# An attention and feed-forward kernel whose result is stored tile by tile, with a new order of its instructions

## The chip, the cores and the metric

The kernel runs on one core of one Trainium2 chip. The core has five engines that work side by side, each on its own stream of instructions: TensorE (PE, matrix products and transposes, with PEld for its weight loads), VectorE (DVE), ScalarE (ACT), GpSimd (POOL) and SyncE (SP), which here only issues transfers. The metric is the device time of one execution in microseconds (us), taken as the median of several runs. The kernel before takes 428.0 us (three runs: 428.0, 427.61, 428.92).

## What is computed

Eight batches of 512 tokens with 512 features pass a cross-attention to 64 memory tokens and then a gated feed-forward block of width 2048, both with a residual. Every linear of the block quantises its input by rows to 8 bits and its weight to three values:

```python
def _rmsnorm(x, g):
    return g * (x * rsqrt(mean(x * x, axis=-1, keepdims=True) + EPS))
def _act_quant(x):
    scale = 127.0 / clip(max(abs(x), axis=-1, keepdims=True), 0.0001, None)
    return clip(round(x * scale), -128, 127) / scale
def _ternary_quant(w):
    s = mean(abs(w))
    return round(tanh(w / (s + EPS))) * arctanh(s)
def _linear_bit(x, w, g):
    return einsum('bsd,od->bso', _act_quant(_rmsnorm(x, g)), _ternary_quant(w))
def _ffn(x):
    h = silu(_linear_bit(x, w1, g1)) * _linear_bit(x, w2, g2)
    return _linear_bit(h, w3, g3)
x = x + _xattn(_layernorm(x), ctx, mask)     # softmax(scores) @ ctx, masked
x = x + _ffn(_layernorm(x))                  # x: 8 x 512 x 512 float32
```

## The kernel before, in words

A batch is four tiles of 128 tokens (tokens on the 128 partitions, 512 features each). A tile goes through these steps, and the names are those that the profile shows:

- Input. `load_x` (lines 473 to 485) brings `mem`, `both` and `x`, 1 MB for a batch, on the queue SP.
- Attention, first half, `pre`: statistics of each tile (`st`, lines 560 and 562), small columns (567), the normalised `t` (582 on ACT or 586 on POOL or DVE), its half-precision copy `xh` (590 on ACT, 591 on DVE) and the remainder (592), a transpose to `xT` (298), and the scores `psc` (602). The maximum is taken off the scores (628 and after).
- Attention, second half, `expo` and `post`: exponential, sum (659), two half-precision parts of the weights `ph` (668 on ACT, 669 on DVE), their transpose to `pT` (298), the product `po` (683), and the addition to `x` (691).
- Quantised input, `quantise_x`: the centred `xm` (721, 725), its squares (731), times the gain (`z`, 736), largest value (741), columns of scales (749 to 766), the two quantised halves (799 on ACT, 800 on POOL or DVE), and the transpose to `zT` (298).
- Feed-forward, `up` and `gate`: for each tile two halves of 1024 columns. `linear` (883) makes `p` in PSUM from `zT` and the weights `w1T` or `w2T`, eight matmuls of 128x512 for a half. SiLU into `h` on ACT (899), the product with the second linear on DVE (927), squares on ACT (932), gain on POOL or DVE (940), then largest value (964), columns (968 to 976), quantisation of `h` (997 on ACT, 999 on POOL), and two transposes to `hT` (1002).
- Down projection, `down_quarter`: 16 matmuls in four quarters into `pd` (825), the addition `x` <- `pd` on DVE (835), and the store. The very last tile goes through `down_last` in two halves of the columns (854, stores at 866).

The transposes `xT`, `zT`, `pT`, `hT` and `mT` are DMA transposes and stand on the queue SP with all loads and stores (for batch 0, and for the last tile, PE transposes instead, and DVE or ACT copies the result out at line 309). An instruction on SP waits for its source at the head of the queue, and everything behind it waits with it.

Before the batches stand the weights: `load_w`, `measure_w` (353, mean of the absolute values), `arctanh` (434), and `quantise_w` (386 on ACT, POOL or DVE; PE transposes; the copy to `w1T`, `w2T`, `w3T` at 390 on DVE, four for each weight).

The program is a plan: `op` notes for each step which engine may do it, what it reads and what it writes. `up` calls `between` four times a tile, where one quarter of the down projection of a tile three places back (`LAG = 3`) and pieces of the attention of later batches (`during`) are noted. The order in which the steps are at last issued, and the engine of each step that has a choice, come from the string `ORDER`, which packs a list of 16-bit codes: the step's number times four, plus the way chosen. `Plan.order` unpacks it, and the loop at the end of the kernel issues the steps one by one; each engine executes its own in that order. Buffers of SBUF and PSUM are assigned by the same order: nine 1 MB buffers `big` hold weights, `x` and `h`; PSUM has three buffers `mm` for `p`, `po` and transposes, one `o` for `pd`, one `a` for `psc`.

The store before, for a tile that isn't the very last, is at lines 839 to 842: the batches 0 to 6 are stored whole, after their fourth tile, and the tiles 0 to 2 of batch 7 one by one.

Of the kernel before, what the change touches and what calls it, by code (L numbers as in the profile page):

```python
# [87 lines left out]
class Plan:  # L88
# [19 lines left out]
    def op(self, engine, cost, run, writes, reads, table=None, other=()):  # L108

        me = len(self.ops)
        deps = set()
# [6 lines left out]
        for b, part in map(pair, writes):  # L120
# [28 lines left out]


ORDER = """
c-jTQedKy+q5$yo@|^eQob#M>o^#G~UY3@Y?~m_~mM$$_y0o;kv@~?-($LV*(9*qHS{k~vG&D4{S3{SEhW==1XlUqOEnONKS{fQ!8d_R
f`lF@cem)c>QkVi1q!1OQa#WtmQU!`oMe2nrQ4#8uDpMg<p<+~=s!|CmNu{VXm7(g?h3-;Ux=r<{4%MJ;G^9VFn$&>8^oJCphZLbl)KB
QIs2bI$BlOqQXH=A4QFnSkPpCEZhMrOz>R;$BHKS(ikp3k-r{2;TdPnW47@egL)RZ03-%}GdPUq+oHKxy0p8h*^p%V0+dQewtLMQ1TsV
V)Wzo3^a#XxpWQ*?p;mIh3b7MT(a8N>j3L1RXw-=p{Roc*3AOvpr-1O0nuNmu9$^C!AWpXey_!mMb-PPqkprr%*Ubed_<Ev7~{=~pJkZ
0Ri1qA~lR+jN|%(;Yg&beSYW*c4M>a!i{E*)DzLip+}b(F-QR9=Ir51R3xy^M>s(HRc0m!@S4TnI7}X_L&$vWJ};b**!O4TA;z?K^#n&
&zKqaCG$R00DopWU?}$3-?42lWV&F)WWk#4vtKhgFl7ep$Kb$p_&!)MBQ^ozY>OX&HS-12VaM#JV8b@qEz@PMpv||~5m<vUn1LO$Wko^
aCZG(COj`I0GY1J42|qA@W0LF!U?Ihh#2x#0Ce3DqP|vVX$g(t>74FQF*@7IK6CTW-&9i_lu<r;vP-HL6ci_NEY>7RxW%k5Y*n%(xXZF
HY*(10}PjF=mTv0fI8(U-VY@L0uG4Nz7;2rJ^y22a&p8@13um?9#1!e9eA+E>)`2z0Xw*Ye~PzM99!oB4l0Dv?&aaB$PPbtPNK%A>_ge
wV45OPB<#X%6^5QuVft}HY_f;)3>xSmiEk{kv^Xo6pHRiVUPI09CH;#yo^7zrWBa#yL!i*f`2uFV~U92W%(?#k7<SN<rxfF<_|R$PbsB  # L160
}egRsliclL|=0UzQzxPE%$p)<N^O8oP-#^6}#LUdBeTRJ09{+zR!&XN<jQXXbL?J2zx#zr}-Oa^E>X&J(N(0^J_6KKe&z9<wHKhzo=^=
%lG&sAK~Xhf`4*Rekj)ksOI<-KjQLyLn!haf$&42z>m3=^eRq;_xKWj;?v?n_#I#8D`JK3^Plofe!_LcwKU>q!XNpiu#sv)34P8d<drb
yqvH2`SBwZV{wy@a8$ac5%8Qtk@5)p7nxFGnEs1~Q-wG*t!T(HH^G$T;FG5@dVp-hqq7s$P{FZ<4P#MVyk&-AeE{S4HxbR8wA&zAzUIi
jH#gsUa3sPK&sX3`7hT=_#t9RiS!c%-zcOp^$A^Z;?5!+}iHlz=Qw(ufVq;G_s&=J~VUTR86-3v)!DZNTn=_noLln|2+;#`V}C;292#J
!jok78Dwi0`N;aVi$XAH<nxh#gcxTdANH#f4;xWz<4dloQYLT`H<j-bqNgihmW~RjVSBKS%$k?xlxx7i;1ag>p@*i#HKSJuxEN(nr!vh
SCg0Wl`#jL>h=UIU)7rP(l)x=VDD>iVJZi-sOy(lp<0~p2~HpE;r=0e34U9T1v}TIG0y)QNqfvq>}WI`_hL}TPjPhN>(CrSzX9ixg&*2
Oxdaf={t!iznAAqMCnOcxuWLesM1ina#dX@Z8-{uQd7yxDWxFil(aID{#(i@9i=aK<gz@Kwn|r7$}?#o$F(M`$O&zyY~+?wmACR(+AD9
AfzpCE*oOt>Tlo%qN?tiAOXVqNbV^C<M`ZwCAW(Afr0mqVvX>J|Q7$U4@Tu%oQ7b8Z<y|=st4awbmG_i{`o8jO1;CnekSTbANv*E56{v
l#i116)hC>Cykz&B9V#6`?;7mEg2b{pH{+SZO3q;xzifRP@#Guqr<<ylDQKRZcIjC#ptfaK08iz4BR8ug8x>gz{;8jVf8TF!+VMZINSv
3QbFsDw{u^KUE))3aziB*B2mW5bLs|DD%(pnWpv<0leqgq$z*3|k4)?o)`wGo`c9=xhE*i@rhPMgDmwm?O=REc&{=h|0lRXeLoxPoJ?0  # L170
axnhYC|t-6Rn}H;Z5DZnYz&S@T9fWwR(UL?V_HwwmMgP>Jiqoi~iK^YF?{reU;M3`a^AMPnFVMwSoE#>{;K!7j0nuL7i&9)7n~7k7+<(
YfCMvU$lw7(^pzYn`wKitmX8LCh9NxN9tC4)puGJMGdI$^@85gUW~og(%;oO#zBjtiZ<1OwnSI`sLl1fo<LpgW38yCQ4OuoK>If%hYnT
-mGp!DiT0iz(`Wk8s-uTK)ZW*t`c-@CBdv=*GHzPWC>eGAu61;zxAh(x=rz5suTc`+^sY|yzJc`{%A<u2QNyg8OTDM}Q4!V5ve7_yv_Y
ThuLd%PsAAl8${6W2V}w?E+8CpOvC-?spY)-D(EuIwlO8hwI_o2YLIotEszFfPc%YOqb+&rK*rFY37zn9G(wG`!BWs4}N3=&X<AC0vjd
MnEb7kzDxr2>Y^f1;&!rU1f<ELor#L&;s-pQGw`80rWMa0OPWAlQbd9pG_28+hTpiE>goTr&JW=_tSm`(G0ls7&!n#RE(=2r$~wT*9#q
&YYC#?CC5cV}rFjlZCi@q_VK1DHkgYV6H|fh}y7%!3)4cOzmpEMmQwM>C6W#@ULRB`dVr=Bqh1TV~8mSUKD=KQ`lf*F2e@m<c_pr}VNF
v4Ax&o7T{}SShP&rOc5zvcAM2zFH5bgVScxD&mZp#}S;h($@c)bF*d*&4u-axiL$4ZPu-f)x~GCY%Z<5wJ@XB*4*HgRj^*H9$uOYe6xy
H%PQcDSv4zG*ID8|zM4;`V<qv;Y+Ds`Y^^Y~?xtvMth@Ca>lGtwh__b7{kipO?W_;no>RtA9JgxtVXmzz9^t+-z`wv-JjRs!u%h<U+Tj
WYZrpycpP0fDe!&2%7~vEy*$ErthF!K}IE@KD;HG`EYwi)Z>^QFD(3!Y<+`vh@iCcJWPw~*6;I<9yh%>{l_Qp=zqI<%3dyUUH?xbw!?%
gXE?Hj)1ihaQer(^#E*WIz*#!H8?M>eu!Hnyj3%X!D{+65ch8GGgy?TMYWR}ONg_80b-_Q3hhox8uW+m2^1?5#a?4$jdH?U56)tM<|9*  # L180
-N`_FWiAmIcNK1pWMEEv6t@2so5+0TN}GccW)o;tG#lg4safJ+DW;hbF>@o*-1KQH{)Df=s<#;g7fNp=5(B#({!)y8z<|eoR|~3H+SOX
owZYRpLWZ=IKOi9<m$9tL~`!U!Op+BEmCr_ZplrPo||{mE+)h&J7u@%v`N>!yK6T?D$c--xF0wnIg`3mAjIvvQTL5IAaC6w>9|9;;f&m
koAjE_kZj!xp~=pT5|8A)lvg4n@^A|t^2X%p=E#y1y$Z>a7lJ)NN?w`7T#>BF$Q!%Fi@Ph*AyxA4WJ79BjWo#AOSoIo@V+IX_h&Npnq=
i2$jpn7rZ*uiZ|!ZpDd~C@zvsP@wzu<sK{{TS{G3$%e<GiFSCS-s67hNjcqx+fY41kvMDmVg?xnq`_aG+%y|TCW1|IS&-i!AnLvP_tJn
Ub*S1;zxNZiYKDSzozy<dA9@8Hcz&O3Sw67gGp+CO=}^={tTi}?w!?p;0NXZ*MR!EgI_Z|mp$xZm*~-j5#b1Apvi{m@VNHNWfce9^!9M
<4n<KkDE7sh<c=e&5ggg&-Nc_!Ix^&-`*w@aKLpDEeRdU;7RJKm5JF@+-l+e$#*WpZfphm;Gum^3%c7uLWzL3NC&o*!Z&m1li#3Hv=)q
1tb^;Fff93&<Z9&JHSCScnNU03Fbj0Bw;5AgKiKBJ`VmEd=e~zT@VdlgJm!bQo%kL1?lh*<b&^nQt-Fn9^8UNI0%#BBcQ`)z=cv+4>I8
}Yy_h)8^UlJyo9+h7L3DkxC&4>3Ae%9Fdm$Od{_x*;WRu4^Dq`(f-qc!)vy*e!g|;YTVXuxhN-X}_QF4eg|Htk!(zAzOW`WqhU@SU?!t
X|3{T-X{D0au@s|
"""  # L190
# [8 lines left out]
def kernel(  # L199
# [620 lines left out]
    def down_quarter(state, q):  # L820
        b, c, hT, f, po = state

        def run():
            for n in range(q * NH // 4, (q + 1) * NH // 4):
                T.matmul(  # L825
                    po(), hT()[:, n * P : (n + 1) * P], w3T()[:, n, :],
                    start=(n == 0), stop=(n == NH - 1),
                )
# [9 lines left out]
        view = out[b].rearrange("(p c) d -> p c d", c=NC)
        if b == B - 1:
            op(DMA, (475, 650, 600), lambda: Q.dma_start(view[:, c, :], xt()[:, c, :]), [], [(xt, c)])  # L840
        elif c == NC - 1:
            op(DMA, (475, 650, 2000), lambda: Q.dma_start(view, xt()), [], [xt])
# [301 lines left out]
```

## Time and profile before

| | |
|---|---|
| median of 3 runs | 428.0 us |
| profiled execution | 427.9 us |
| its span in the trace | 425.8 us |
| mean granted TensorE clock | 0.987 |
| instructions in the trace | 6677 |
| HBM read and written | 25.76 MB, 8.39 MB |

The profile is one execution; its span is shorter than its time by 2.1 us, which lie outside the recorded work. The page gives, for each engine, the time in which it was busy, then the span in 40 slices of 10.6 us with the busy share of each slice in tenths (9 is 90% or more). Two of these rows show how the run is staged: in the first seven slices the weights are loaded and quantised, after which PE is full to the end, and DMA is fullest at the start:

```profile
PE   0563878999999999999999999999999999999996
DMA  7999994497555578863589635864644546533272
```

Then come the costliest groups of instructions: line, engine, operation, tiles out and in, shapes, count; total busy us and mean ns of one; and the idle time of that engine just before them, with what ended most of it. These are the ones that the order moves between engines, or that the added stores wait for:

```profile
L940 POOL TENSOR_TENSOR h<-h,g_bc 128x1024 f32<-128x1024 f32 x55 | 130.4, 2377 | 2.7 <-ACT sq L932 2.1
L997 ACT ACTIVATE h<-h,hf 128x2048 f16<-128x2048 f32 x23 | 45.8, 1994 | 0.2 <-DVE hf L968 0.2
L592 POOL TENSOR_TENSOR xh<-t,xh 128x512 f16<-128x512 f32 x32 | 37.3, 1168 | 2.0 <-DVE xh L591 1.2
L799 ACT ACTIVATE xm<-z,zf 128x512 f16<-128x512 f32 x42 | 28.1, 709 | 0.7 <-DVE zf L760 0.7
L835 DVE SCALAR_TENSOR_TENSOR x<-pd,hf,x 128x512 f32<-128x512 f32 x31 | 23.1, 744 | 3.0 <-PE pd L825 2.6
```

### The profile page before, as it was taken

What the parts mean: (1) busy time and instruction counts of PE and PEld (TensorE: products, weight loads), DVE (VectorE), ACT (ScalarE), POOL (GpSimd) and SP (SyncE); (2) the same over time, 40 slices, a digit from 0 to 9 for tenths busy, and PEclk for the clock granted to TensorE, in tenths of its full rate; (3) what the DMA queues carried; (4) which work ended last, traced back from release to release, by engine and by line L of the source; (5) the groups of instructions that cost most, each with busy time, mean ns of one, the idle gap of its engine ahead of it and who ended that gap; (6) DMA issues with size and microseconds to landing.
All of it is one profiled execution on the core that took longest, in us unless ns stands there. A gap on an engine that the chain in (4) does not pass through costs nothing.

```text
span 425.8 us, 6677 instructions
## 1 busy us (share of the span) xinstructions
PE 388.8 (91%) x2174; PEld 192.8 (45%) x2174; DVE 369.0 (87%) x832; ACT 341.3 (80%) x464; POOL 368.7 (87%) x330
## 2 busy tenths in 40 slices
PE   0563878999999999999999999999999999999996
PEld 0341534544444544454445444544454444444444
DVE  4689999999998998799989998999789888897772
ACT  1799999979899799598996898988686986774531
POOL 1789998998999999699999999999699979988650
PEclk9996899999999999999999999999999999999999
DMA  7999994497555578863589635864644546533272
GB/s 217 408 406 376 380 208 52 103 255 147 126 112 150 99 131 157 183 174 68 104 158 276 136 76 82 171 174 83 134 76 148 75 87 146 152 77 73 49 207 90
DMA packets 142514, 67.35 MB, mean 158 GB/s; under 512 B 133136, under 2 KB 133520, under 8 KB 140048
## 3 DMA queue, kind: packets, MB, share of 16 engines
q1 hardware_dynamic: 142480, 66.93, 63.4%
q8 instruction: 17, 0.28, 0.3%
q14 instruction: 17, 0.14, 0.1%
HBM read 25.76 MB, written 8.39 MB: 80 GB/s over the span
## 4 chain that ended last, share of the span: by engine, by line
PE 78%; DVE 6%; POOL 6%; DMA 3%; issue 3%; ACT 2%; SPq 0%; DVEq 0%; POOLq 0%; ACTq 0%
PE p L883 48%; PE pd L825 24%; PE po L683 3%; DMA zT<-xm 2%; PE psc L602 2%; POOL tq L386 2%; DVE st L560 1%; DMA both<-in_ctx_dram 1%; PE pd L854 1%; POOL t L586 1%; POOL xh L592 1%; POOL mv L291 1%; DVE zf L741 1%; DVE h L927 1%; ACT h L899 1%
## 5 line engine op out<-in xcount | busy, mean ns | idle before, releaser
L883 PEld LDWEIGHTS <-zT 128*128 128x128 f16 x1024 | 99.5, 98 | 122.0 <-issue 3.0
L940 POOL TENSOR_TENSOR h<-h,g_bc 128x1024 f32<-128x1024 f32 x55 | 130.4, 2377 | 2.7 <-ACT sq L932 2.1
L883 PE MATMUL p<-w1T,zT 128*128 128x512 f16 x512 | 120.4, 383 | 2.4 <-DVE zT L309 1.5
L883 PE MATMUL p<-w2T,zT 128*128 128x512 f16 x512 | 119.2, 379 | 1.1 <-DVE h L927 0.9
L825 PE MATMUL pd<-w3T,hT 128*128 128x512 f16 x496 | 117.8, 379 | 0.0
L927 DVE SCALAR_TENSOR_TENSOR h<-p,zf,h 128x1024 f32<-128x1024 f32 x64 | 81.9, 1280 | 14.9 <-PE p L883 8.4
L899 ACT ACTIVATE h<-p,zf 128x1024 f32<-128x1024 f32 x64 | 70.1, 1105 | 24.8 <-PE p L883 17.0
L932 ACT ACTIVATE sq<-h 128x1024 f16<-128x1024 f32 x64 | 67.2, 1050 | 17.0 <-DVE h L927 14.8
L825 PEld LDWEIGHTS <-hT 128*128 128x128 f16 x496 | 47.9, 98 | 55.6 <-DMA hT<-h 0.2
L964 DVE TENSOR_REDUCE hf<-h 128x1 f32<-128x2048 f32 x31 | 70.6, 2278 | 1.8 <-POOL h L940 1.7
L736 POOL TENSOR_TENSOR z<-xm,g_bc 128x1024 f32<-128x1024 f32 x29 | 69.8, 2423 | 1.4 <-ACT xm L725 0.6
L997 ACT ACTIVATE h<-h,hf 128x2048 f16<-128x2048 f32 x23 | 45.8, 1994 | 0.2 <-DVE hf L968 0.2
L741 DVE TENSOR_REDUCE zf<-z 128x2 f32<-128x1024 f32 x32 | 38.8, 1211 | 5.8 <-POOL z L736 5.7
L592 POOL TENSOR_TENSOR xh<-t,xh 128x512 f16<-128x512 f32 x32 | 37.3, 1168 | 2.0 <-DVE xh L591 1.2
L799 ACT ACTIVATE xm<-z,zf 128x512 f16<-128x512 f32 x42 | 28.1, 709 | 0.7 <-DVE zf L760 0.7
L731 ACT ACTIVATE xsq<-x,xf 128x512 f32<-128x512 f32 x32 | 22.9, 715 | 6.5 <-DVE x L691 6.0
L835 DVE SCALAR_TENSOR_TENSOR x<-pd,hf,x 128x512 f32<-128x512 f32 x31 | 23.1, 744 | 3.0 <-PE pd L825 2.6
L691 DVE SCALAR_TENSOR_TENSOR x<-po,mx,x 128x512 f32<-128x512 f32 x32 | 22.9, 745 | 1.3 <-PE po L683 1.2
L602 PE MATMUL psc<-mT,xT 128*128 128x128 f16 x256 | 19.7, 224 | 1.9 <-DMA xT<-xh 1.9
L560 DVE BATCH_NORM_STATS2 st<-x 128x6 f32<-128x512 f32 x32 | 21.3, 679 | 0.0
L602 PEld LDWEIGHTS <-xT 128*128 128x128 f16 x256 | 16.9, 101 | 8.5 <-DMA xT<-xh 3.5
L291 POOL TENSOR_TENSOR hf<-hf,neg_half 128x1 f32<-128x1 f32 x32 | 20.1, 634 | 0.2
(134 smaller groups left out, 483.4 us busy)
## 6 DMA issues: line engine op xcount, KB each, us to landing
raw<-in_L_ffn_w_dram SPq DMA_DIRECT2D x10, 1024.0 KB, 13.8
x<-in_x_dram SPq DMA_DIRECT2D x7, 1024.0 KB, 6.9
out_dram<-x SPq DMA_DIRECT2D x7, 1024.0 KB, 4.1
mem<-in_ctx_dram SPq DMA_DIRECT2D x16, 128.0 KB, 6.5
w3T<-in_L_ffn_w_dram SPq DMA_DIRECT2D x2, 1024.0 KB, 12.6
both<-in_ctx_dram SPq DMA_DIRECT2D x4, 256.0 KB, 8.2
x<-in_x_dram SPq DMA_DIRECT2D x2, 512.0 KB, 6.1
g_bc<-in_L_ffn_g_dram SPq DMA_DIRECT2D x1, 1024.0 KB, 14.9
```

What stands on the lines that cost most here:

```text
L592: rest = lambda e, t=t, xh=xh: e.tensor_tensor(xh()[:, 1, :], t(), xh()[:, 0, :], ALU.subtract)
L602: T.matmul(psc()[:, c, :, :].rearrange("p s m -> p (s m)"), xT()[:, k, :], mT().rearrange("p (s d) m -> p d s m", s=2)[:, k % ND, :, :], s ...
L736: gain = lambda e, xm=xm, z=z: e.tensor_tensor(z(), xm().broadcast_to([P, 2, D]), g_bc(), ALU.mult)
L741: lambda i=i, z=z, am=am: V.tensor_reduce(am()[:, i, :], z(), AX.X, ALU.max, apply_absolute_value=True),
L825: T.matmul(po(), hT()[:, n * P : (n + 1) * P], w3T()[:, n, :], start=(n == 0), stop=(n == NH - 1),)
L883: T.matmul(ps()[:, k * HC : (k + 1) * HC], zT()[:, g * ND + d, :], weight(d, j * HW // HC + k), start=(d == 0), stop=(d == ND - 1),)
L899: lambda: A.activation(h()[:, j * HW : (j + 1) * HW], ps(), AF.Silu, scale=fac()[:, 0:1]),
L927: lambda: V.scalar_tensor_tensor(cols(), ps(), fac()[:, 1:2], cols(), ALU.mult, ALU.mult),
L932: lambda: A.activation(sq(), cols(), AF.Square, scale=(RMS / H) ** 0.5, accum_out=col(j)),
L940: run = lambda e: e.tensor_tensor(cols(), cols(), g3_bc()[:, j * HW : (j + 1) * HW], ALU.mult)
L964: lambda: V.tensor_reduce(col(2), h(), AX.X, ALU.max, apply_absolute_value=True),
L997: op(ACT, 1995, lambda: A.activation(hq(), h(), AF.Copy, scale=col(5)), [h], [(f, 5)], other=[(POOL, 1970, lambda: G.tensor_scalar(hq(), h ...
```

## The change

Two things change. In `down_quarter` every tile is stored on its own, 256 KB from the 128 partitions, for all batches; and the string `ORDER` is another one. The store of a tile waits for that tile's addition at line 835, and its place on the queue SP comes from the new order. The added stores are 21 steps more in the plan.

```diff
 ORDER = """
-c-jTQedKy+q5$yo@|^eQob#M>o^#G~UY3@Y?~m_~mM$$_y0o;kv@~?-($LV*(9*qHS{k~vG&D4{S3{SEhW==1XlUqOEnONKS{fQ!8d_R
-f`lF@cem)c>QkVi1q!1OQa#WtmQU!`oMe2nrQ4#8uDpMg<p<+~=s!|CmNu{VXm7(g?h3-;Ux=r<{4%MJ;G^9VFn$&>8^oJCphZLbl)KB
...
+c-jTQf8@G(f&lR6$NTyHety57-|r6%9Ssc)&FM}@Lth%&)6&q=($SZOhK81omWGCgmYkM`hL(nghK7!YhK7#*XldwZXlQ9xdm0*A`lID
+uFM{BSFaZciXaph(M4reJ6(U092$zTwWg<qDh!9aE;shoVM3SfyDFTv+ypV0;Ms|q~(IZ^4PoxQr%n$<tlXW6Q4v88uBEBKQ<dqze4dP
...
 """
...
         view = out[b].rearrange("(p c) d -> p c d", c=NC)
-        if b == B - 1:
-            op(DMA, (475, 650, 600), lambda: Q.dma_start(view[:, c, :], xt()[:, c, :]), [], [(xt, c)])
-        elif c == NC - 1:
-            op(DMA, (475, 650, 2000), lambda: Q.dma_start(view, xt()), [], [xt])
+        op(DMA, (475, 650, 600), lambda: Q.dma_start(view[:, c, :], xt()[:, c, :]), [], [(xt, c)])
```

From line 839 on, line numbers after are three lower than before (927 becomes 924). What the new order assigns otherwise, by lines of before, in instructions before and after:

| Engine | Fewer | More |
|---|---|---|
| DVE, 802 to 791 | 669: 3 to 0; 663: 20 to 16; 760: 46 to 40; 766: 46 to 38; 591: 7 to 4; 979: 25 to 22 | 567: 8 to 16; 592: 0 to 2; 800: 2 to 4; 940: 9 to 11; 586: 0 to 1; 309 of pT: 1 to 2 |
| ACT, 355 to 360 | 799: 42 to 40; 725: 17 to 16; 309 of pT: 1 to 0 | 668: 4 to 7; 590: 25 to 28; 997: 23 to 25; 582: 20 to 21 |
| POOL, 335 to 335 | 940: 55 to 53; 586: 12 to 10; 592: 32 to 30; 999: 8 to 6 | 760: 9 to 12; 766: 9 to 13; 976: 7 to 10 |
| SP, 191 to 212 | stores of 1 MB: 7 to 0 | stores of 256 KB: 3 to 31 |

(The counts are of the built program, where a step of several small instructions counts each.) PE has the same matmuls in another order: between the last linear and the first transpose of the last tile, for one, stand 60 down matmuls before and 40 after.

More of the change, by code (lines that the diff above doesn't have):

```diff
@@ L151 @@
 ORDER = """
[L152 to L186, printed above, removed]
@@ L187 @@
-1tb^;Fff93&<Z9&JHSCScnNU03Fbj0Bw;5AgKiKBJ`VmEd=e~zT@VdlgJm!bQo%kL1?lh*<b&^nQt-Fn9^8UNI0%#BBcQ`)z=cv+4>I8
-}Yy_h)8^UlJyo9+h7L3DkxC&4>3Ae%9Fdm$Od{_x*;WRu4^Dq`(f-qc!)vy*e!g|;YTVXuxhN-X}_QF4eg|Htk!(zAzOW`WqhU@SU?!t
-X|3{T-X{D0au@s|
+c-jTQf8@G(f&lR6$NTyHety57-|r6%9Ssc)&FM}@Lth%&)6&q=($SZOhK81omWGCgmYkM`hL(nghK7!YhK7#*XldwZXlQ9xdm0*A`lID
+uFM{BSFaZciXaph(M4reJ6(U092$zTwWg<qDh!9aE;shoVM3SfyDFTv+ypV0;Ms|q~(IZ^4PoxQr%n$<tlXW6Q4v88uBEBKQ<dqze4dP
+p(NsNgV@i8$b@8pD76GQS{a!PE7H_0tABbM}ld_~TQx5x~+Blg7GWR{%K2cl2L$sdU+og?#Pf;<ru@=PSjUx+DrA@0PJoRM>qpsvJ&n9
@@ new lines @@
+v0h(%+DPdJ;TUBnc8y8dV|@<x)JkBYz~9Bp{~@rXJ*q%usvsHQA&>RE5k_uc#AQCI5#EQ#CR|HOM-N=qPm{=X8u}l4o*5W+{zsk#VX`C
+a5jhAs2LuDo|b0rQ1}F!gP`<Qb(ps^~nFALUfAiP#da8y{4+vM^u=O(F>|iy-5$LI`tXVVmsgiDg(Zx+H4+-sW}y;3!n&w^pyI9Zcts&
+0&!3RJ-Q9{)PK@FFk?p4nE#qu(ce-Xwohllit2+VodXH5rUqb5kLUq?p!Uq?phb7+Ej0ogdQ8v2fyr`Xum(Ho3bu5do`5d>12|F%x(s;
+kCu$Co^k1kP2e}lT<~HDGDoyX`3I7X~p)*`k&C(i2(ogD6<!Hoh!Jd9ldHOB@`h9K(4z$1&Xo0>^MfymW=o4Mwrl3rp=_9Dn7rIJcg(N
+62SGq<Qxf7_<H#!FHbOpT6K;{hIWd8xW+zsqO6_goXEHWDNpf&Nt+`&fxF?H~y-(o7v1EjzO5CDk)q(PM#Ffk_1EI^HMnG&}Im`N~0Cd
@@ new lines @@
+8x|9)y`WlVr-=o6MPMfF4)jAZP-YdylDdB}M}mW(5eQ#q_y4lVy(FjwM(G0MlkhT#mUiE?6*QuF7Hn#SmCBVX$I4Oa$D7C}=Pb;T4lo*
+UX+humkS*%!c9Fcf<)7;hyZCud!VQun;Ch%r&_ahuA3FXI%Eo^%#P?Gif#{-Wb5eSjcXf9rMqu#y*&o*kv>9mdEUlPswwx$0pe<8)Bc#
+nwyAWw$6p+1e;@1?1;&;4X(&;xB@%m#>|%63NijQJLO93iOuj6ro#S?ZLkZj%74!G*(TfNcfyFRai6hEZZFKZ9{(kq7FXPb3vn~H%#Yc
+h*&7?-r)*p6^A-LrE+g`A&VI`-Sb~qr0Iu04|4&?2{Em%rJRjvZY=XbDKeAhPDiXp)O!8;;Dn8g09~B_q;(-8oUYLm*e_=6y<&r|0pNl
+sx&fU3^kl@;Uh>r<Vz9#IsPq;9Tq#6G)_u%GyOl}ErVZr}{OUn^CBX_tCzvPo#LD+F^;lQo<4WE?{{7BmfalWgixQ_6loDeR;iC+mtp}
@@ new lines @@
+^OLBkxKFp~$a=n|S6+e3rlPIo{&${6u>SHTfvK&%1m_!%|NJ;#hm~Q;iVUd|m#TukpX|f7TlEU*rcr;OqQOTZ#={6Gl81WMRmM1SGiPU
+ITJU=!#Dfiwz+ygoS}{5?mo75>iu)iXm|*M1+{w6mnuq%!>;#BizNT&=!Z{O5BPSAtb#PMnYEr(yxV{P!+xxBT`=2i)*nU_JyWA7Q*6J
+!bJF5c!+Z$Dutzll#|xdPr|3-LWoIusV6Rlj#Lyk(r4mP>Pj22FP`O+SdbF1ES{vAI1-c6Kq^Teh$$%v8)8cyi)X1P)y1-uR)^9=x=20
+PmJi~G;z&A*Cy|#jY8n2!0;PAPKGY;$-bxv%BArDjU*xoOl_pS!Atft~rJEF1uJQv`r3yswF4ZI#Hl^Q66*UFxQdx~Cb@+q>IE5|gU3~
+$=upwcXRU@!1g<wwA<hS4w_NAOMl~!;e&7`@Mlb2EqBKdt~B@wbKhvb7+Rk0kG<8UY4<b#xy6LLY>OC>o2(=abTq&zIZvOJfwu&fcVA{
@@ new lines @@
+XQad`e4sAur7$j4L^~meYDyKA1CDQkt*?6G~A&nk~3CJ8~5kl{SnjKq)ID_&L1GYxpVL!7=R1dwC8wFsW3OEsQA-xuzVo8vI^fDIMi0^
+Ga8#E8odGr3(+RCpVO}vWFY_sq~a19LOg)l=sRN4%CCZl?n9*k$N(ra+D|X9TEz!x#~>Tl%F70k+N2+imOcJwDLE2HV4Ye{FA&fQ_2@I
+KpSPKW|TiFCuO7@l#mM4o4Qet%2sJAV<oJfm701{u1ZadsCV^arJ+XEjNVp8>P^|I1?{e6^_C8`p@Nl@_E7ffL}{u;?JMPLrK0t<vo=@
+iT3zK)RePu{^%M0E>Zj^JgUHnuN<-sStnJjEI@M<yRA;)ThP1ZcS4-M|t8;CvF4T)Q*Oy98pQtf)sy5I;UFdy1p=w%O9UC!ip$!eBAJv
+&UGCKM|ziKV*TeYjZdR`CfNL#5II;leqp|g5XpXySNYYA<o5n5A=Xe%9PVXcYQT2xzVJw2%vbgXZ*vVPHvdP-aCL;Y7;TrV1TZKKEZoc
@@ new lines @@
+4wuGD><y&ub6uVne5HT=lDZvu|3-Na#=Pq2KhK&g%^$X6*Hd9yXFX)FVdIh#NaY)2n(^PZ$S%tEUX$?2U+7(|M<^PmH@g(lzI5f1wk`N
+l%%7*C%?^Y#9x`Yycx|K8>i+)Q|d8Pa8=iXYj^Z&loWW855H*Uum)d%=fgs(Kcp=Yy8UCno}cV77X63m~%rn^6J9CM$haR1+}PtYmj=@
+{LUz;jNUbN=E3Nj&~#DFTpJZ5i{cJOXVgM9V`B`>m{~QhMh@l7x;Zu5=x8j^#k?DN^JHv|gtJ5gb7mIIt64P{<^`RNhjBBy=w>!d&HTO
+jvDq_5X4||N$Q+vwv_gGjV|Pr~yrR81Fvd<8^-$M*m@j71dBg0WxcM}HYlhGo_0bmntNC}cWG2lb+S+-vLpKyQ=jISq(G%@a*_=4M^&2
+!o5wx?Th_L!r38fqY6|8{;tqLk5%^IT(Dq1o0FQ|s@D2`&*zoDufvQj8)MXbC%Ky{Qx6Es6pD}xI5S19e&>?5jJ$oc`zEZ5TA6DnC%>n
@@ new lines @@
+&?;JuP5it6`O`Z>*seu@lzRA?%tpbAED`)*N-LxD~ZC&eE=1No!>_t+lnck-N8AR?2#1t?aIKv_7$VR@ORL58HJQcE-9`z|L7u`)d8o$
+vP+N>YS~kjhwu7vrhKSN!YG4vL4pMnOJvgY+>8CH<n<(VMDuUKb@ql*$roF)$Onyc6SzbQZ}+1cGGFv5jSSforROOTQ+t(&U<#>4mnx7
+W4G<Dy|$N5$?n;Ar);0?fn9K-ZpF^ogcG+1PT1KxA@>s};<UV&yK=H_)EU};bXIQH$+;uD?dILJ`=woU#&*&D%5Hl@r{}bsj@x%<_Rbk
+O5pV4b+_|0i_D<A0It%;PPTBpz8M=Ar;0i8q-*wY&!GrE^+>LW`M()wgxP&|KdTz<7xF>hwPTiUNp)+?0ujpO8p|@~fJ2hwIec;61l6!
+Wm?%n&yUAhVPckar&dUc2Q#~$xB+@#xep+9z;?!zm2TesyxukG(#;O*UaytTLSGTz2bdat~ToA3($)qQ#&cquRI-Q1X0^fhnmS>Dd`yq
@@ L190 @@
+W*M9`-tZ)g%0zSN7(9$U}b3t9wVU;f1|FcpdM*JlFrm>w9x=;x)a4xAC#R^rl|S5BW3i=577E3;ekMa5ewwmi>g^@WVmfulf~#=ZF1)p
+Y&h(Dc=pUe#CG3H9zW4g7<tJ<ou!E^7nqp&->FL63l~>H}a#w*#FW`2WRg)e-SMGslWE$4idrt`G560!PQR&nV|1?gMN?=N<r7p1pp6%
+n?DR5LC>!Q%V6O@gM<I4z{NaX1xG)OA%6HLzZ_uveb5W;{yrE7hd{%#U>!toJ*ePw&<HNUCICScSA%0v$J^lPp8_JN1y%fWkitUH3_?K
+zr|~W5;<s@Vw}N;8gA8urdoaK~+zzt%eVoIopp6T-h_85v^FaxZ@C_G&JJy0Pa1AeT8Bg#McW@uCFbdZA&v=8s$5Xt=#o&QYc!m#nj-Q
+yoKVsqqydccKgzy=|mkW;L=t}}?FG(DGK`;2leTly$UP3S7m&nWi1E<;hKL
 """
```

## The prediction

> **What bounds the kernel now.** I read the busy table first, then windows of time, then PE's waits, then the queue SP, the only one to which the change adds instructions.
>
> ```profile
> PE 388.8 (91%) x2174; PEld 192.8 (45%) x2174; DVE 369.0 (87%) x832; ACT 341.3 (80%) x464; POOL 368.7 (87%) x330
> ```
>
> Shares over the whole span hide two stages. The windows before and after 80 us (busy us of PE, PEld, DVE, ACT, POOL) part them:
>
> ```profile
> 0.00:80.00 80.00, 47.68 (x427) 30.87 (x428) 67.38 (x191) 65.59 (x86) 61.81 (x76) 0.94 0.86 275
> 80.00:420.00 340.00, 338.88 (x1731) 160.23 (x1730) 300.65 (x640) 275.73 (x378) 306.90 (x255) 1.00 0.59 132
> ```
>
> After 80 us PE is busy 338.88 of 340 us: only 1.1 us can be won there, and whatever makes PE wait is lost in full, since the same matmuls stand behind it. Before 80 us PE idles 32.3 us and DVE is the fullest engine. The waits of PE and of its weight loads from 100 us on name what is nearest to the path:
>
> ```profile
> PE p L883 <- DMA zT<-xm: 1.1, 2, 0.9
> PEld L883 <- DMA zT<-xm: 2.0, 3, 1.1
> PEld L602 <- DMA xT<-xh: 0.6, 2, 0.4
> PEld L825 <- DMA hT<-h: 0.2, 1, 0.2
> ```
>
> So the first linear of a batch waits for zT, the transposed quantised input, which ACT makes (line 799) and SP transposes. One such place, at the start of batch 4, in the timeline of SP and then of PE:
>
> ```profile
> 223.26 0.52 SPq L485 DMA_DIRECT2D x<-in_x_dram  x1
> 227.21 0.36 SPq L842 DMA_DIRECT2D out_dram<-x  x1
> 230.00 3.97 SPq L298 DMA_TRANSPOSE zT<-xm  x2
> 235.67 1.90 PE L883 MATMUL p<-w2T,zT 128*128 128x512 f16 x8 [0.19 <-DMA zT<-xm]
> ```
>
> Two transposes that elsewhere take 2.60 us together (186.89, below) took 3.97 with a 1 MB load and a 1 MB store before them. The stores' own rows, and the place of the other critical transposes:
>
> ```profile
> out_dram<-x SPq DMA_DIRECT2D x7, 1024.0 KB, 4.1
> zT<-xm SPq DMA_TRANSPOSE x28, 3.2
> out_dram<-x SPq DMA_DIRECT2D x3, 256.0 KB, 2.5
> 168.99 1.19 SPq L298 DMA_TRANSPOSE pT<-ph  x1
> 186.89 2.60 SPq L298 DMA_TRANSPOSE zT<-xm  x2
> 190.17 1.90 PE L883 MATMUL p<-w2T,zT 128*128 128x512 f16 x8
> ```
>
> The last two lines are batch 3: issued 186.89, landed 3.2 us later at 190.1, used at 190.17. There is no slack at that place.
>
> **The change part by part.** *The stores.* 7 stores of 1 MB, 3 of 256 KB and 2 of 128 KB become 31 of 256 KB and 2 of 128 KB: 21 instructions more on SP at 0.33 to 0.58 us of issue, 7 to 12 us spread over 290 us. SP mostly waits for its sources in that time, so the issue itself costs nothing as long as the store's source is done; if it is not, whatever stands behind is held. The bytes are the same 8.39 MB. From issue to landing, the 7 large stores take 7 x 4.1 = 29 us and the 28 small ones in their place 28 x 2.5 = 70 us by their rows. If those 41 us were paid one after another, the time would be 428 + 41 = 469. I do not add them, for nothing on chip reads what is stored: the landing of a store releases only its buffer of x and a DMA semaphore. A rule of the Trainium skill (DMA: Bandwidth & Descriptors, Rules for kernel authors) speaks against the change: it wants at least 1 MiB for each DMA and many small transfers joined into a large one. By that rule the loss would be near the 41 us of the rows; it is a rule for bandwidth, and the DMA engines are 0.59 busy in the window after 80 us.
>
> *The gain of splitting.* With 256 KB in front, the pair of zT at 230.00 would take 2.60 in place of 3.97: up to 1.4 us there, of which PE can gain only what it waited (0.19, and 0.7 at its weight loads). The other wait, 0.9 us at 102.66, has no store before it. In the new order the store of batch 2's last tile stands behind both zT of batch 4, so that gain I expect; it is at most 0.9.
>
> *The wait that is added on SP.* Each store waits for the addition at line 835 on DVE. In the new order the store of tile (1, 2) stands ahead of hT of (2, 0) and pT of batch 3; before, it stood behind them with the whole batch. In the old trace that addition ran at 169.52 to 170.3, and pT was issued at 168.99. The new DVE stream has about as much in front of that addition (169 to 171), then 0.35 for the store, 1.3 for hT: pT goes out at 171 to 173 and lands 2.4 later, 173 to 175, while PE wants it at 174.5. Price: 0 to 0.9; I take 0.5.
>
> *The new order, start.* The way to PE's full stage runs over DVE up to its last copy of w3 (line 390, twelfth). Counting the instructions ahead of it with the old rows' durations: 80.05 us before (187 instructions), 81.75 after (196). More: eight one-column operations at line 567 (1.14), three at 749 (0.43), a reduce at 659 (0.41), a half-wide subtraction at 592 (0.65), pT 0.28, two small ones 0.35, which is 3.26; less: three at 434, two at 760, one 591, one 562, which is 1.56. Neighbours overlap by 0.08 (two 0.68 at line 560 take 1.28), so nine more instructions give 1.70 - 0.72 = 1.0 us. Against it: the last slice of w1 is now measured by ACT in one pass of 2.08 beginning when it lands (20.1), not in two halves with the exponential between them, which ended at 23.26; the mean comes about 0.7 us earlier. DVE idles 2.3 us between 30 and 80 us, which can hide some. Sum +0.3; bounds -1.0 (all hidden, and the gain stays) to +1.7. The subtraction on DVE has no row of its own: 0.43 (cast of the same width, line 591) to 1.17 (POOL's own), within these bounds.
>
> *The new order, full stage.* PE does the same matmuls; the order moves work between the others. POOL gives away about 10 us (two gains at 940, two 1971 ns quantisations, two subtractions, two at 586); ACT takes 4.8. What matters is ACT's sum ahead of the critical zT: up to the first of batch 3, 174.9 before and 176.4 after, +1.4; up to the first of batch 4, 218.0 and 220.9, +2.9 (three casts at 590, four at 582, one at 668, one 725; less one 997, one 731, one 310). ACT's neighbours overlap by 0.10 (four 0.709 at line 799 take 2.55), so +1.2 and +2.3. At batch 3 there is no slack: +1.2. At batch 4, 2.3 less the 0.9 of the split store leaves 1.4, and PE comes there 0.8 earlier in its list: 2.2; ACT's own waits before it (1.45 at 227.65) take back up to half. I take 1.7 for the later of the two, bounds 0 (ACT idles 16 us between 100 and 240 us, and all of it is absorbed) to 3.5 (nothing is). These do not add up: a PE that is 1.2 late at batch 3 finds batch 4 that much readier, and the 0.5 of the SP wait is in it too. So 1.7 in all.
>
> *The end.* Before, 60 down matmuls stand between the last linear and the first transpose of the last tile, 13.0 us at 0.216 from one start to the next; after, 40, 8.6 us. What they cover: multiply 1.29, square 1.25, gain 1.29, reduce 1.21, an addition 0.75, four small 0.7, half a quantisation 1.7, which is 8.2. Price 0; if DVE arrives 1 us late, 0.6. The last two stores are the same 128 KB ones.
>
> Sum against the profiled execution: 427.9 + 0.3 + 1.7 = 429.9; the median of the runs stands 0.1 above it (428.0): **430.0 us**. A measurement of this kernel can tell about 0.3% (1.3 us) from no change.
>
> **The rivals.** *The cover holds (no change).* ACT's idle time swallows the late zT, and only the start counts: 428.0 + 0.3 = 428.3. For it: every engine but PE has 10% or more idle time after 80 us. Against: that idle time is waiting for inputs, and 190.17 has no slack. *The split frees the transposes (faster).* At each batch's start zT no longer queues behind 1 MB, PE's waits of 0.9 and 0.9 vanish and the start takes its lower bound: 428.0 - 1.9 - 1.0 = 425.1 at the best, 426.5 likely. It decides if ACT makes zT of batches 3 and 4 no later than now. For it: 3.97 against 2.60. Against: there is only 1.1 us of PE idle time left to win. *SP held at its stores (much slower).* 28 stores (four in each of seven batches) wait on DVE with transposes behind them; if once a batch the addition is late by more than the 1 to 2 us of slack seen for pT and zT, seven batches at about 1 us each give 428.0 + 7 = 435. It decides where SP waits longer for line 835 than zT, pT or hT behind it can spare.
>
> **How the numbers follow.** Forecast (small waits) 0.48; SP held 0.16; no change 0.16; faster 0.20. With start and zT at their bounds the forecast's sum runs from 428.0 - 1.0 + 0 = 427.0 to 428.0 + 1.7 + 3.5 + 0.6 = 433.8; what of it lies below 429.3 I count as no change, so its own range is 429.3 to 433.8. The range over all cases takes in the likely part of the faster rival (426.5) with half a microsecond, and of the rival with SP held its 435 and one more for a late start: 426.0 to 436.0. Slower 0.48 + 0.16 = 0.64, same 0.16, faster 0.20.
>
> **What would show it.** Right: PE busy below 338 us in the 340 us after it fills, with new waits of "PE p" for "DMA zT" near batches 3 and 4 and of "PE po" for "DMA pT" near 175; ACT ending its zT later; the twelfth w3 copy on DVE at 80.5 to 81.5 us. Wrong: PE full from before 79.5 us, or no zT wait of over 0.5 us (rivals one and two); SP waits for DVE x at line 839 of several us with PE idle behind each (rival three); or PE waiting for PSUM buffers held by DVE at line 927, which this sum leaves out, for DVE's total grows by under 2 us.

## The result, and the profile after

The changed kernel takes 431.45 us (median of 5 runs, 430.48 to 431.9) beside 428.81 for the kernel before (5 runs). The ratio is 1.0059, 95% interval 1.004 to 1.0077: slower by 2.5 us, of which the interval leaves 1.7 to 3.3. The forecast was 430.0, slower by 2.0.

First the busy table of the changed kernel, whose profiled execution has a span of 428.7 us (2.9 more than before):

```profile
PE 391.8 (91%) x2174; PEld 194.2 (45%) x2174; DVE 372.8 (87%) x821; ACT 345.7 (81%) x469; POOL 359.2 (84%) x330
```

Then the same two windows as before (busy us of PE, PEld, DVE, ACT, POOL, then granted clock, DMA share, GB/s):

```profile
0.00:80.00 80.00, 49.33 (x419) 31.70 (x420) 67.26 (x197) 64.10 (x85) 59.12 (x70) 0.91 0.85 274
80.00:420.00 340.00, 337.19 (x1720) 158.74 (x1718) 303.07 (x622) 281.58 (x385) 300.06 (x261) 1.00 0.61 131
```

PE was busy 338.88 of the 340 us after 80 us and is busy 337.19: its idle time there grew from 1.12 to 2.81 us, 1.7 us in this execution. The matmuls are the same. POOL gave away 6.8 us there, ACT took 5.9, DVE 2.4. The rest of the 2.9 us lies in the start: the twelfth copy of w3 on DVE, which opens the full stage, begins at 80.51 in place of 79.28. The waits of PE from 85 us on, in the timeline (start, length, then in brackets the idle time before the group and what ended it):

```profile
103.66 3.63 PE L880 MATMUL p<-w1T,zT 128*128 128x512 f16 x16 [0.83 <-DMA zT<-xm]
123.96 1.90 PE L880 MATMUL p<-w1T,zT 128*128 128x512 f16 x8 [0.16 <-DMA zT<-xm]
221.17 1.04 PE L825 MATMUL pd<-w3T,hT 128*128 128x512 f16 x4 [0.73 <-DMA hT<-h]
235.43 2.75 PE L825 MATMUL pd<-w3T,hT 128*128 128x512 f16 x12 [1.01 <-DVE x L835]
```

The first wait was there before (0.93 at 102.66). The last two are new, and both stand around the start of batch 4, where the forecast had looked for the loss; but they wait for hT and for the addition at line 835, not for zT. After 260 us PE is full.

Last, the queue SP at that place, and the stores from issue to landing:

```profile
225.80 0.53 SPq L485 DMA_DIRECT2D x<-in_x_dram  x1
...
233.07 2.60 SPq L298 DMA_TRANSPOSE zT<-xm  x2
235.77 0.52 SPq L839 DMA_DIRECT2D out_dram<-x  x1
```

```profile
out_dram<-x SPq DMA_DIRECT2D x31, 256.0 KB, 2.7
```

The pair of zT of batch 4 takes 2.60 in place of 3.97, and the store now stands behind it: this part of the change does what was expected. The pair is issued 3.1 us later than before, though, at 233.07.

### The profile page after: what moved, and what is told of

It reads as the page before. It is cut to its first block, busy times and chain, and to the rows that moved or that the text cites. A ratio compares the mean times of both kernels' runs of the same rounds, so it can differ in the third digit from the quotient of the medians.

```text
span 428.7 us, 6719 instructions
## 1 busy us (share of the span) xinstructions
PE 391.8 (91%) x2174; PEld 194.2 (45%) x2174; DVE 372.8 (87%) x821; ACT 345.7 (81%) x469; POOL 359.2 (84%) x330
## 4 chain that ended last, share of the span: by engine, by line
PE 58%; POOL 11%; DVE 10%; ACT 8%; DMA 7%; issue 4%; SPq 1%; POOLq 0%; ACTq 0%; DVEq 0%
PE p L880 36%; PE pd L825 18%; POOL z L736 3%; POOL h L937 3%; DMA mem<-in_ctx_dram 2%; DMA xT<-xh 2%; PE po L683 2%; ACT w2T L353 2%; DVE zf L741 2%; ACT h L896 2%; DMA zT<-xm 2%; DVE z L736 1%; POOL tq L386 1%; PE psc L602 1%; DMA hT<-h 1%
## 5 line engine op out<-in xcount | busy, mean ns | idle before, releaser
L937 POOL TENSOR_TENSOR h<-h,g_bc 128x1024 f32<-128x1024 f32 x53 | 126.6, 2398 | 10.9 <-ACT sq L929 10.5
L880 PE MATMUL p<-w1T,zT 128*128 128x512 f16 x512 | 122.4, 386 | 1.1 <-DMA zT<-xm 1.0
L994 ACT ACTIVATE h<-h,hf 128x2048 f16<-128x2048 f32 x25 | 49.9, 1995 | 4.2 <-DVE hf L965 3.9
L592 POOL TENSOR_TENSOR xh<-t,xh 128x512 f16<-128x512 f32 x30 | 36.3, 1213 | 4.8 <-DVE xh L591 4.3
L799 ACT ACTIVATE xm<-z,zf 128x512 f16<-128x512 f32 x40 | 26.8, 709 | 1.3 <-DVE zf L760 1.1
L590 ACT CAST xh<-t 128x512 f16<-128x512 f32 x28 | 16.9, 610 | 3.8 <-DMA xT<-xh 3.6
```

What stands on the lines that cost most here:

```text
L592: rest = lambda e, t=t, xh=xh: e.tensor_tensor(xh()[:, 1, :], t(), xh()[:, 0, :], ALU.subtract)
L799: by_act = lambda to, from_, by: A.activation(to, from_, AF.Copy, scale=by)
L880: T.matmul(ps()[:, k * HC : (k + 1) * HC], zT()[:, g * ND + d, :], weight(d, j * HW // HC + k), start=(d == 0), stop=(d == ND - 1),)
L937: run = lambda e: e.tensor_tensor(cols(), cols(), g3_bc()[:, j * HW : (j + 1) * HW], ALU.mult)
L994: op(ACT, 1995, lambda: A.activation(hq(), h(), AF.Copy, scale=col(5)), [h], [(f, 5)], other=[(POOL, 1970, lambda: G.tensor_scalar(hq(), h ...
```

## The experiments

All ratios are to the kernel before in runs on the same chip, with their 95% intervals. The changed kernel's own is 1.0059 (1.004 to 1.0077).

**Stores and order apart.** Two kernels take the change to its halves. In the first, the new order has the old stores:

```diff
-        op(DMA, (475, 650, 600), lambda: Q.dma_start(view[:, c, :], xt()[:, c, :]), [], [(xt, c)])
+        if b == B - 1:
+            op(DMA, (475, 650, 600), lambda: Q.dma_start(view[:, c, :], xt()[:, c, :]), [], [(xt, c)])
+        elif c == NC - 1:
+            op(DMA, (475, 650, 2000), lambda: Q.dma_start(view, xt()), [], [xt])
```

> The new order with the old stores: the first three stores of a batch are gone and the 1 MB store stands at the place of the fourth. Theory A (the order alone costs the time: 1.3 us in the start and 1.7 us around batch 4, both where VectorE's two-operand multiplications from SBUF meet a running GpSimd instruction): no change against the changed kernel, 431.4 us, 2.6 over before. Theory B (the 28 small stores cost it, for SP is held at them): 428.8, as before. Theory C (small stores help the transposes behind them, as the forecast had it, by up to 0.9): 432.0 to 432.3.

Measured: 431.25 us, ratio 1.0059 (1.0038 to 1.008). The loss is there without one added store.

In the second, the old order has the new stores, each right behind its addition in the list of steps:

```diff
 addition of tile (b, c) at line 835
+store of tile (b, c), c < 3
 ...
-store of batch b
+store of tile (b, 3)
```

> The old order with the new stores: each of the three added stores of a batch is put right behind the addition of its tile, the fourth where the 1 MB store was. Theory A: as before, 428.8 us. Theory B: 431.4, or more, since nothing searched for the places of the stores. Theory C: 427.9 to 428.5.

Measured: 429.61 us, ratio 1.0007 (0.9991 to 1.0024). Both say the same: by the second, the split stores cost at most 1 us and gain at most 0.4; no difference was found. Theory B falls, and theory C has nothing to show.

**Start and rest apart.** After 480 steps (stores not counted) the two orders have issued exactly the same set, so they can be joined there.

```diff
 ORDER
-steps 1 to 480 of the new order
+steps 1 to 480 of the old order, with its engines
 the other steps in the new order
```

> The first 480 steps (all of the weights, up to the second down projection, some 95 us) in the old order, the rest in the new one, with the split stores. Theory A: the start's part goes, 431.45 - 1.35 = 430.1 us. If the lateness of the start is made up later: 431.4. If all of the loss sits in the start: 428.8.

Measured: 430.78 us, ratio 1.0039 (1.002 to 1.0059).

```diff
 ORDER
-steps 1 to 480 of the old order
+steps 1 to 480 of the new order, with its engines
 the other steps in the old order
```

> The counterpart: the first 480 steps in the new order, the rest in the old one with the whole stores. Theory A: 428.8 + 1.35 = 430.1 us; with the one before, the two losses add up to that of the changed kernel. If the start doesn't count: 428.8.

Measured: 429.32 us, ratio 1.0008 (0.9993 to 1.0022). So the new rest costs 0.0039 x 429 = 1.7 us (0.9 to 2.5) and the new start 0.3 (-0.3 to 0.9). Theory A had 1.35 for the start, read off one pair of profiled executions, and that was too much. The last window of the start (60 to 80 us; the third number from the right is the granted clock), before and then after, shows why:

```profile
60.00:80.00 20.00, 16.49 (x144) 10.06 (x145) 19.48 (x50) 19.10 (x25) 17.59 (x18) 1.00 0.42 74
```

```profile
60.00:80.00 20.00, 17.09 (x144) 10.64 (x145) 19.47 (x50) 19.64 (x27) 17.68 (x18) 0.91 0.40 78
```

The window holds 144 matmuls in both, and they took 0.6 us more of PE in the execution of after, whose clock was at 0.91. That is no property of the order: of the four profiled executions with the old start (leaving out the two kernels of over 450 us below) three had 1.00 in this window and one 0.91, of the seven with the new start four and three. Over these eleven the last copy of w3 starts at 79.28, 79.63, 80.15 and 80.77 us with the old start and at 79.90 to 81.13 with the new one, in the mean 79.96 and 80.47.

The traces also show where the new start is late. On SP a 1 MB load of weights now stands ahead of the second half of the memory tokens of batch 0, and ScalarE waits for them:

```profile
12.94 1.28 ACT L533 ACT_TABLE_LOAD   x1 [12.94 <-DMA mem<-in_ctx_dram]
```

Before, that wait ended at 8.53. The mean of w1, with which its quantisation begins, is on DVE at 24.98 us in place of 23.71; over the eleven executions at 25.18 in the mean with the new start and 24.39 with the old one.

**The lock between VectorE and GpSimd.** The trace of after has a length that no count of instructions would give. The timeline of DVE, and then of POOL, at batch 4:

```profile
226.72 3.17 DVE L736 TENSOR_TENSOR z<-xm,g_bc 128x1024 f32<-128x1024 f32 x1
229.92 1.22 DVE L741 TENSOR_REDUCE zf<-z 128x2 f32<-128x1024 f32 x1
...
234.63 0.74 DVE L835 SCALAR_TENSOR_TENSOR x<-pd,hf,x 128x512 f32<-128x512 f32 x1
```

```profile
226.43 2.37 POOL L937 TENSOR_TENSOR h<-h,g_bc 128x1024 f32<-128x1024 f32 x1
```

DVE's gain multiplication took 1.21 us in the start of the kernel before. Here, for tile (4, 1), POOL's began 0.3 us before it and ended at 228.80; DVE's ended 1.09 us after that, as if it had only then begun. The addition at 234.63, for which PE waited 1.01 us, is queued behind it. In the kernel with the old stores DVE came first, by 0.12 us; its timeline of DVE and of POOL:

```profile
226.72 1.25 DVE L735 TENSOR_TENSOR z<-xm,g_bc 128x1024 f32<-128x1024 f32 x1
```

```profile
226.84 3.34 POOL L939 TENSOR_TENSOR h<-h,g_bc 128x1024 f32<-128x1024 f32 x1
```

Now POOL takes the longer time, by 1.0 us; DVE's still needed 1.1 when POOL's began. In five profiled executions with this multiplication in the new rest, PE waits for the addition behind it in the three where POOL began first (1.0, 1.1 and, with the quantisation on ScalarE, 2.4 us), and not in the two where DVE did. The same step, measured alone:

```diff
+for pool in (False, True):
+    for form in FORMS:
+        if pool:
+            for _ in range(6):
+                G.tensor_tensor(gc[:], ga[:], gb[:], ALU.mult)
+        for _ in range(4):
+            form()
```

> No part of the reference is computed: six forms of VectorE instruction of 128x1024, four of each, first alone and then beside six GpSimd multiplications of 128x1024; x is read and a product is stored in the place of the result. Theory A: beside GpSimd, the forms with two SBUF operands (tensor_tensor, and scalar_tensor_tensor from SBUF) take up to one GpSimd instruction longer, 1.2 to some 3.5 us; scalar_tensor_tensor from PSUM, the reduction and the form with an accumulated output stay as they are alone, within 0.05 us. If the cause is another (bandwidth of SBUF): all forms grow by a similar share.

The timeline of DVE, four instructions a line: first each form alone, then beside POOL.

```profile
6.91 5.00 DVE L87 TENSOR_TENSOR c<-a,b 128x1024 f32<-128x1024 f32 x4 [0.72 <-DMA b<-in_x_dram]
...
11.95 5.01 DVE L88 SCALAR_TENSOR_TENSOR c<-a,b 128x1024 f32<-128x1024 f32 x4
...
16.98 5.00 DVE L89 SCALAR_TENSOR_TENSOR c<-ps,b 128x1024 f32<-128x1024 f32 x4
...
21.96 4.97 DVE L90 TENSOR_REDUCE sums<-a 128x1 f32<-128x1024 f32 x4
...
31.90 2.87 DVE L92 TENSOR_SCALAR half<-a 128x1024 f16<-128x1024 f32 x4
...
34.75 9.03 DVE L87 TENSOR_TENSOR c<-a,b 128x1024 f32<-128x1024 f32 x4
...
53.33 11.19 DVE L88 SCALAR_TENSOR_TENSOR c<-a,b 128x1024 f32<-128x1024 f32 x4
...
71.65 4.99 DVE L89 SCALAR_TENSOR_TENSOR c<-ps,b 128x1024 f32<-128x1024 f32 x4
...
86.48 4.97 DVE L90 TENSOR_REDUCE sums<-a 128x1 f32<-128x1024 f32 x4
...
116.14 9.05 DVE L92 TENSOR_SCALAR half<-a 128x1024 f16<-128x1024 f32 x4
```

Two operands from SBUF: 5.00 becomes 9.03 and 5.01 becomes 11.19. One operand from PSUM: 5.00 stays 4.99; the reduction stays at 4.97, and the form with an accumulated output at 1.22 for one. The plain conversion to f16, which theory A had not on its list, goes from 2.87 to 9.05. So not all forms grow by a similar share, as they would by sharing bandwidth, and theory A's mechanism, one instruction waiting for the other, is right; its condition, two operands from SBUF, is too narrow. What it costs this kernel is another matter. The next two take it away, with the form that does not wait:

```diff
+ALONE = ((4, 1),)
...
+alone = lambda xm=xm, z=z: V.tensor_scalar(
+    z(), xm().broadcast_to([P, 2, D]), 1.0, 1.0, ALU.mult, ALU.mult, accum_out=sink())
...
-other=[(DVE2, 1215, lambda gain=gain: gain(V))])
+other=[(DVE2, 1215, alone if (b, c) in ALONE else lambda gain=gain: gain(V))])
```

> The changed kernel, with VectorE's gain multiplication for tile (4, 1) replaced by one that reads a single SBUF operand (times 1.0, with an accumulated output that nobody reads); that tile's gain g is left out. Theory A (that multiplication waits for a GpSimd instruction, 3.17 us in place of 1.21, and PE's wait of 1.01 us for the addition behind it is the consequence): it takes about 1.2 us in every execution, the wait goes, and the time is 431.4 - 1.0 = 430.4. Theory D (the loss is many small waits of the new order, and this is one that falls in some executions only): 430.9 to 431.4.

Measured: 431.23 us, ratio 1.0047 (1.0034 to 1.006). Its profiled execution has no wait for the addition any more, but 0.90 for hT at 222.66, 0.60 for zT at 193.09 and 0.56 for pT at 176.60.

```diff
-ALONE = ((4, 1),)
+ALONE = ((0, 2), (4, 1))
```

> The same for tile (4, 1) and for tile (0, 2) in the start, where the multiplication took 2.88 us; the gain of both tiles is left out. Theory A: the first one's 1.0 and, of the start's loss, what the runs with old and new starts showed (0.3 to 0.7): 429.7 to 430.1. If the start's lateness has another source (the late memory tokens): as the run with tile (4, 1) alone.

Measured: 431.44 us, ratio 1.005 (1.0037 to 1.0064). Theory A's 1.0 us did not come: the point estimate fell by 0.5, which the intervals can't tell from nothing, and freeing the second lock, in the start, gained nothing more. This agrees with theory D: the wait is one of several, and in the two traces the others are larger when it is gone. That they grow because it is gone is not shown by one trace each.

**ScalarE's load.** The wait for hT at 221 has tile (3, 0) behind it, whose quantisation the new order gives to POOL. Moved back:

```diff
-quantisation of h of tile (3, 0): GpSimd, line 996
+quantisation of h of tile (3, 0): ScalarE, line 994
```

> The changed kernel with one instruction moved back: the quantisation of h of tile (3, 0), which the new order gave to GpSimd, runs on ScalarE again, as in the kernel before. Theory E (its transpose hT is late because GpSimd takes it late: PE waits 0.3 to 0.7 us at 221 in all three executions of the new order): that wait goes, 430.7 to 431.0. Theory of the forecast (ScalarE's sum ahead of the zT of batch 4 decides): 2.0 us more on ScalarE there, 432 to 433.4.

Measured: 432.62 us, ratio 1.0086 (1.0059 to 1.0113), against the 1.0059 of the same order without the edit. The waits of PE around batch 4:

```profile
219.90 1.04 PE L825 MATMUL pd<-w3T,hT 128*128 128x512 f16 x4 [0.24 <-DMA hT<-h]
235.45 2.75 PE L825 MATMUL pd<-w3T,hT 128*128 128x512 f16 x12 [2.37 <-DVE x L835]
```

PE waits 0.24 for hT in place of 0.73, as theory E said, but 2.37 for the addition in place of 1.01. In this execution (430.75 us, the fastest of its six) PE comes to the place 1.3 us earlier than in the one of after, and the addition at 234.66 comes no earlier. What holds DVE ahead of it shows first in DVE's timeline, in the changed kernel and then with the quantisation on ACT:

```profile
222.75 0.21 DVE L749 TENSOR_SCALAR zf<-xss 128x1 f32<-128x1 f32 x2 [0.91 <-ACT xsq L731]
```

```profile
223.86 0.21 DVE L749 TENSOR_SCALAR zf<-xss 128x1 f32<-128x1 f32 x2 [2.81 <-ACT xsq L731]
```

DVE idles 2.81 us for the squares on ACT, which stand behind the added quantisation, and its additions of batch 4, its gain and the addition that PE wants are queued behind that. But the lock is in it too: DVE's gain multiplication took 2.92 us at 226.99, POOL's having begun at 226.48. The trace doesn't part the two. The counterpart takes ACT's load down:

```diff
-t of (4, 0), t of (5, 0): ScalarE, line 582; ph of batch 3: ScalarE, line 668
+t of (4, 0), t of (5, 0): GpSimd, line 586; ph of batch 3: VectorE, line 669
```

> The changed kernel with three instructions taken off ScalarE again, in the new order: the normalisations of tiles (4, 0) and (5, 0) go back to GpSimd and the first half of ph of batch 3 to VectorE, 2.0 us less on ScalarE ahead of batch 4's zT, 1.5 more on GpSimd, 0.3 more on VectorE. Theory of the forecast (ScalarE's sum decides): the time falls by 1.0 to 1.7, to 429.7 to 430.4. Rival (all three engines stand at their limit there, what one gains another loses): 431 to 432.

Measured: 430.73 us, ratio 1.004 (1.0024 to 1.0056). Between the two edits lie 4.0 us of ACT work, and 0.0046 x 429 = 2.0 us of time, whose intervals don't meet. Each alone overlaps the changed kernel's interval. So at this place ACT's sum counts, for about half of what it is by the two ratios. The share is not shown more closely: the same edits take 2.0 us off POOL and put 1.5 on it, and in the trace of the second DVE came ahead of POOL at the lock, 1.38 us for the multiplication.

**Engines and sequence.** Does the loss come from the moves between engines, or from the sequence?

```diff
 ORDER: the sequence of the new order
-each step on the engine of the new order
+each step on the engine of the old order
```

> The new order, but each step on the engine that the old order gave it, with the split stores. If the moves between engines cost the time: 428.8 to 429.6. If the sequence itself costs it: 431.4. If order and engines only fit together: above 432.

Measured: 452.44 us, ratio 1.0537 (1.0511 to 1.0563). The largest waits of PE from 85 us on (us in total, times, longest):

```profile
PE p L880 <- DMA zT<-xm: 8.3, 6, 3.7
PE pd L825 <- DVE x L835: 3.8, 4, 2.5
```

```diff
 ORDER: the sequence of the old order
-each step on the engine of the old order
+each step on the engine of the new order
```

> The old order, each step on the engine that the new order gives it, with the whole stores. If the moves between engines cost the time: 431.4. If the sequence costs it: 428.8 to 429.6. If they only fit together: above 432.

Measured: 456.39 us, ratio 1.0596 (1.0556 to 1.0636). Neither alone is the cause of the 2.5 us: each of these two sequences is good for its own engines only, and crossing them costs 23 to 26 us, some ten times what the two good pairs differ by.

**Where the rest loses.** PE is full from 260 us on in the changed kernel, so a kernel that changes to the new order at some 245 us should be as good as the old one:

```diff
 ORDER
-steps 1 to 1224 of the new order
+steps 1 to 1224 of the old order, with its engines; each store right behind its addition
 the other steps in the new order
```

> The old order for the first 1224 steps (to some 245 us, into batch 4), each store right behind its addition, and the new order with its stores for the rest. If the loss lies around batches 3 and 4, as the traces show (TensorE is full from 260 us on in every run): as the old order with split stores, 429.0 to 429.6, end of the kernel included. If the later part costs something too: 430 or more.

Measured: 430.54 us, ratio 1.0034 (1.0017 to 1.0051), 1 us over what was expected. Its interval still overlaps that of the old order with the split stores (0.9991 to 1.0024), but lies above the kernel before. Its waits of PE after the joint:

```profile
263.29 1.89 PE L880 MATMUL p<-w1T,zT 128*128 128x512 f16 x8 [0.34 <-ACT h L896]
283.02 3.63 PE L880 MATMUL p<-w1T,zT 128*128 128x512 f16 x16 [0.55 <-DMA zT<-xm]
```

Neither is in the trace of the changed kernel, where PE comes to the second place at 283.35, 0.3 us later still and without a wait. The second is in two other traces of the whole new rest, with 0.35 and 0.19 us. So the new order has too little slack in more than one place, and a PE that is already late can hide the later ones. That it hides them all is not shown, and the joint itself, which neither order was made for, may cost a part.

## Why the prediction was right, point by point

- *Slower, by 2.0 us: right.* 2.5 (1.7 to 3.3). The rivals "no change", "the split frees the transposes" and "SP held at its stores" (428.3, 426.5, 435) all lie outside the runs' interval of 430.5 to 432.1 (428.81 times 1.004 and 1.0077).
- *Issue of 21 stores and their landing cost nothing: right.* 1.0007 in the old order, and no difference with and without them in the new one. SP waits 47.6 us in total for line 835 at 14 of the stores in the trace of after, without a measured cost. The rule of the Trainium skill (DMA: Bandwidth & Descriptors, Rules for kernel authors) for transfers of at least 1 MiB, which spoke against the change, is not borne out here: of the 41 us by which the landings are longer, the interval in the old order leaves at most 1.0.
- *The gain of splitting, at most 0.9: the mechanism right, the gain not there.* zT of batch 4 took the forecast 2.60 us, but with the store behind it. With 256 KB in front, as in the old order with the split stores, it took 3.02, so the forecast's 2.60 was too low for that case. It was also issued 3.1 us later, and the wait that it would have removed was replaced by others.
- *The wait added on SP, 0.5: the time right, the cause wrong.* pT of batch 3 goes out at 172.64, within the forecast 171 to 173, and PE waits for it 0 in the execution of after and 0.56 in that of the freed multiplication. But in the new order with the old stores, where no store of that batch stands ahead of it, pT goes out at 172.03. The chain comes from ACT: its exponential (line 645) runs at 169.66 in place of 166.52, and at 169.04 with the old stores, 0.6 earlier like pT itself. So it is part of the order's term, not of the stores'.
- *The start, +0.3: right in sum, and by luck.* 0.3 by the joined kernels (-0.3 to 0.9), 0.5 by the mean start of the last copy of w3. But the term that made it small, a mean of w1 that comes 0.7 us earlier, has the wrong sign: the last pass over w1 on ACT began at 22.43 in the trace of after, not at 20.1, and over the traces the mean came 0.8 later. And DVE's gain multiplication of tile (0, 2), counted with the old row's 1.2 us, took 2.4 to 2.9 in all six traces of the new start that have it. DVE's idle time between 30 and 80 us, which was to hide some, is 1.7 us by its window (48.34 busy of 50), not 2.3. Why the sum still comes out, and what absorbed these, no run shows.
- *The full stage, 1.7: right in size* (1.7, 0.9 to 2.5), *half right in place, so the size is in part luck.* At batch 3 zT is late as forecast; the weight loads of PE in the trace of after:

```profile
191.77 11.77 PEld L880 LDWEIGHTS <-zT 128*128 128x128 f16 x56 [0.57 <-DMA zT<-xm]
```

  In five other traces of this rest, PE itself waits 0.34 to 0.60 us there, where the forecast had 1.2. At batch 4 the forecast named zT, and PE waited for hT (0.73) and for the addition at line 835 (1.01) before it came to zT. The step that failed is the one that put DVE aside because its total grows by under 2 us: the addition stands in DVE's queue behind the lock, and a total of DVE's work, in which the multiplication of 3.17 us counts as 1.2, does not show that. How much of the 1.7 this step is worth stays open, since freeing the lock changed the time by nothing that the intervals can tell. ACT's sum, the forecast's lever, counted with about half its weight in the two edits of it.
- *The end, 0: right.* From the start of the last block of down matmuls to the end of the span stand 22.8 us before and 23.5 after. Without PE's work in them (68 and 72 matmuls at 0.216, and in both some 0.9 for 16 transposes and 3.46 for 32 half matmuls) that is 3.8 and 3.6.

Of the forecast's signs, PE was busy below 338 us (337.19) and the twelfth copy of w3 began at 80.51; the waits for zT at batch 3 and for pT near 175 do not stop PE in the trace of after, but do in others of the same rest, some of them with an edit.

What stays open: which of the small waits make up the 1.7 us, and in what shares; and why the new order's times spread a little more (429.8 to 433.5 in twelve runs with the old stores, 427.4 to 430.4 in 35 of the kernel before). The race at 226.7 us, decided by 0.03 to 0.5 us in the five traces, could spread them; there are too few traces of either outcome to say so. The orders of PE and of the other engines were not exchanged one engine at a time.

## What to carry to other kernels

Cost a new order of instructions by the places where the full engine has no slack, not by the sums of the others alone, and don't expect the losses of several such places to add: one reached early can hide the next. Cutting a store that nobody on the chip reads into four cost nothing measurable here, and running either sequence with the other's engines cost 23 to 26 us: move the two together. When a change mixes a small edit with a new order, run the edit in the old order first: that one kernel told the two apart here.
